# Linear attention with a two-part number format: the low half of v times the high half of A as 64-row matmuls

## The chip, the cores and the metric

The kernel runs on one core of a Trainium2 chip. The metric is the device time in microseconds (us). Lower is better. The engines are TensorE (PE, with its weight loads shown apart as PEld), VectorE (DVE), ScalarE (ACT), GpSimd (POOL) and SyncE (SP), which issues all the DMAs of this kernel.

## The reference

One transformer block on x of 4096 tokens x 512 numbers, in fp32:

```python
q = x @ Wq.T   # 16 heads of 128
k = x @ Wk.T   # 4 heads of 128, each shared by 4 heads of q
v = x @ Wv.T
q, k = rope(q), rope(k)
qf, kf = elu(q) + 1, elu(k) + 1
# causal linear attention, token by token:
state += kf[:, None] * v[None, :]
z += kf
out = (qf @ state) / (qf @ z + 1e-6)
x = layernorm(x + out @ Wo.T)
# feed-forward: Hadamard transform, up and gate projections, silu, Hadamard transform, down projection
x = layernorm(x + ffn(x))
```

## The kernel before

**Numbers in two parts.** Nearly every matmul is made of a high and a low part: `hi` is the value rounded to fp32r, the matmul format (an ACT copy, which rounds on writing), `lo` is the rest (a DVE subtraction). A product is then hi x hi + hi x lo + lo x hi, three matmuls that add up in one PSUM bank. The helper `hilo` (lines 89 to 91) does this for inputs and weights.

**Attention** (lines 134 to 488) runs over blocks of 256 tokens, 16 of them, twice: `s` is 0 or 1 and takes two of the four kv heads each time. So there are 32 blocks `n`; a block has two heads `g` and for each two slots `p` of 128 tokens, hence 128 slots `(n, g, p)`. A slot consists of two chunks `c2` of 64 tokens; `c = 2p + c2` is the chunk within its block. A chunk's 256 matmul columns are 4 heads of q times 64 tokens.

- `proj_v` (L192) projects v for a block, takes it out of PSUM as `vhl` (high part by ACT, L198; low part by DVE, L200), and copies it by DMA into `vd`: chunk by chunk, high and low part, once on partitions 0 to 63 and again on 64 to 127 (four DMAs, L202 to L205).
- `proj_k` projects k (L239), rotates it, applies elu + 1, and makes `khl`, the high and low part of each chunk next to each other: 64 columns of high, 64 of low. Column 0 of a chunk is replaced by z, the running sum (L267, L268).
- `proj_q` does the same for q, two heads of q at a time (`qh`, `ql`).
- `nat_k` and `state` transpose k (L277) and make the state before each of the four chunks. `state` (L289) has four matmuls in plain fp32, which the chip runs as two passes each. They take 64, 128, 64 and 128 partitions: the sum inside a pair of chunks starts at its first or second half.
- `scores` makes A, the products of k and q inside a chunk. One matmul has [high | low] of k as its 128 output partitions (L332), so that rows 0 to 63 of the bank get kh x qh and rows 64 to 127 kl x qh; a second one (L333) adds kh x ql to rows 0 to 63. ACT rounds rows 0 to 63 into A (L339), DVE computes what the rounding lost (`am`, L342) and adds it to rows 64 to 127 (L343). So A holds its high half on partitions 0 to 63 and its low half on 64 to 127. POOL then zeroes what lies above the diagonal, half by half (L346).
- `av` adds up the numerator of a slot in a PSUM bank `ps_num` (two banks): for each chunk three matmuls with the state (high x high, high x low, low x high), and two with `vd`. As A holds both halves on 128 partitions and `vd` holds the same v on both, one matmul gives vh x (Ah + Al), and a second vl x (Ah + Al) (L364). A further matmul with a selecting matrix adds up the denominator (`ps_den`, L367). ACT takes the numerator out (L370) and a DMA stores it.

The loop over slots (lines 420 to 486) starts `proj_q` five slots ahead and `scores` one slot ahead. That order is only a first one: the program is built with `tile.TileContext(nc, schedule_with_timeline_sim=True)`, and this scheduler reorders the instructions of every engine by what it reckons to be ready. Matmuls that stand next to each other in the source needn't do so in the program. Pools give the number of buffers: `A` has four, `vd` and `khl` two, `ps_num` two banks.

**After attention** come the output projection with the first layernorm (L622), and the feed-forward (L682 gate and up, L707 down) with the second.

Of the kernel before, what the change touches and what calls it, by code (L numbers as in the profile page):

```python
# [9 lines left out]
F32 = mybir.dt.float32  # L10
F32R = mybir.dt.float32r
# [36 lines left out]
def kernel(  # L48
# [8 lines left out]
    def dma(dst, src, pin=False):  # L57
        if dst.dtype == F32R:
            dst = dst.bitcast(F32)
        if src.dtype == F32R:  # L60
            src = src.bitcast(F32)
        i = nc.sync.dma_start(dst, src)
        if pin:
            tc.keep_in_program_order(i)
# [66 lines left out]
        dma(xn, x_n[t * 128:(t + 1) * 128])  # L131
        cur[t] = dict(nt=nt, rb=rb, xn=xn)

# [1 line left out]
    with ExitStack() as es:  # L135
        early = ExitStack()
        pe = early.enter_context(tc.tile_pool(name="ae", bufs=2, side="right"))
# [45 lines left out]
        def proj_v(n):  # L183
            s, b = divmod(n, NB)
            B = blk[n]
            ps = pmm.tile([128, 2, 256], F32, tag="mm", name="ps_v")
            for t in range(2):
                i = 0
                for k in range(4):
                    for xa, wa in (("xh", 0), ("xh", 1), ("xl", 0)):  # L190
                        w = W["v", s, k // 2][wa].rearrange("p (k d) -> p k d", k=2)
                        T.matmul(ps[:, t], B[xa][:, k, t * 128:(t + 1) * 128], w[:, k % 2],  # L192
                                 start=i == 0, stop=i == 11)
                        i += 1
            v32 = pe.tile([128, 2, 256], F32, tag="v32", name="v32")
            S.activation(v32, ps, AF.Copy)
            vhl = p1.tile([128, 2, 2, 256], F32R, tag="vhl", name="vhl")
            S.activation(vhl[:, 0], ps, AF.Copy, scale=rowm_s)  # L198
            yield
            V.scalar_tensor_tensor(vhl[:, 1], ps, rowm_s, vhl[:, 0].bitcast(F32), ALU.mult, ALU.subtract)  # L200
            vd = p2.tile([128, 2, 4, 256], F32R, tag="vd", name="vd")
            for half in range(2):  # L202
                for par in range(2):
                    dst = vd[half * 64:half * 64 + 64].rearrange("p l (t r) d -> p l t r d", r=2)[:, :, :, par]
                    dma(dst, vhl[par * 64:par * 64 + 64])  # L205
            vs = p1.tile([128, 2, 256], F32, tag="vs", name="vs")
            dma(vs[63:128], v32[0:65])
            dma(vs[0:63, 1], v32[65:128, 0])
            if b:
                dma(vs[0:63, 0], blk[n - 1]["v32"][65:128, 1])  # L210
            else:
                G.memset(vs[0:63, 0], 0.0)
            B.update(v32=v32, vd=vd, vs=vs)
# [30 lines left out]
        def proj_k(n):  # L244
            s, b = divmod(n, NB)
            B = blk[n]
            ps = proj(n, [("k", s, 0), ("k", s, 1)])
            kft = pe.tile([128, 2, 320], F32, tag="kft", name="kft")
            yield from rope(ps, B["csb"], kft[:, :, 64:320])
            if b:  # L250
                S.activation(kft[:, :, 0:64], blk[n - 1]["kft"][:, :, 256:320], AF.Copy)
            else:
                G.memset(kft[:, :, 0:64], 0.0)
            khl = p2.tile([128, 2, 4, 2, 64], F32R, tag="khl", name="khl")
            kh, kl = khl[:, :, :, 0], khl[:, :, :, 1]
            kc = kft[:, :, 64:320].rearrange("p g (c j) -> p g c j", c=4)
            S.activation(kh, kc, AF.Copy)
            yield
            V.tensor_tensor(kl, kc, kh.bitcast(F32), ALU.subtract)
            z = p2.tile([128, 2, 4], F32, tag="z", name="z")  # L260
            dz = p2.tile([128, 2, 4], F32, tag="dz", name="dz")
            for g in range(2):
                V.tensor_reduce(dz[:, g], kft[:, g, 1:257].rearrange("p (c j) -> p c j", c=4),
                                AX.X, ALU.add)
                V.tensor_tensor_scan(z[:, g], ones4, dz[:, g], blk[n - 1]["z"][:, g, 3:4] if b else 0.0,
                                     ALU.mult, ALU.add)
            V.tensor_copy(kh[:, :, :, 0], z)  # L267
            V.tensor_tensor(kl[:, :, :, 0], z, kh[:, :, :, 0].bitcast(F32), ALU.subtract)  # L268
            B.update(kft=kft, z=z, khl=khl)

        def nat_k(n):
# [50 lines left out]
        def scores(j):  # L322
# [5 lines left out]
            for c2 in range(2):  # L328
                c = 2 * p + c2
                t = slice(64 * c, 64 * c + 64)  # L330
                khl = B["khl"][:, g, c]
                T.matmul(ps[:, c2], khl.rearrange("p l j -> p (l j)"), qh[:, :, t], start=True, stop=True)  # L332
                T.matmul(ps[0:64, c2], khl[:, 0], ql[:, :, t], start=False, stop=True,  # L333
                         skip_group_check=True)
            am = p2.tile([64, 512], F32, tag="am", name="am")
            A = p3.tile([128, 2, 256], F32R, tag="A", name="A", bufs=4)
            Af = A.rearrange("p a b -> p (a b)")
            psf = ps.rearrange("p a b -> p (a b)")
            S.activation(Af[0:64], psf[0:64], AF.Copy)  # L339
            B["A", g, p] = A  # L340
            yield
            V.tensor_tensor(am, psf[0:64], Af[0:64].bitcast(F32), ALU.subtract)  # L342
            V.tensor_tensor(Af[64:128], psf[64:128], am, ALU.add)  # L343
            for h in range(2):
                ah = Af[64 * h:64 * h + 64].rearrange("p (a q) -> p a q", q=64)
                G.affine_select(ah, ah.bitcast(F32), pattern=[[0, 8], [1, 64]], compare_op=ALU.is_ge,  # L346
# [2 lines left out]
        def av(n, g, p):  # L349
            s, b = divmod(n, NB)  # L350
            B = blk[n]
            A = B.pop(("A", g, p))
            qh, ql = B["q", g]
            sh, sl, _ = B["S"][g]
            gs = slice(g * 128, (g + 1) * 128)
# [1 line left out]
                B["den", g] = pden.tile([4, 256], F32, tag="den", name="ps_den")  # L357
            den = B["den", g]
            ps = pnum.tile([128, 2, 256], F32, tag="num", name="ps_num")
            for c2 in range(2):  # L360
                c = 2 * p + c2
                t = slice(64 * c, 64 * c + 64)
                ops = [(sh[:, c], qh[:, :, t]), (sh[:, c], ql[:, :, t]), (sl[:, c], qh[:, :, t]),
                       (B["vd"][:, 0, c, gs], A[:, c2]), (B["vd"][:, 1, c, gs], A[:, c2])]  # L364
                for i, (l, r) in enumerate(ops):
                    T.matmul(ps[:, c2], l, r, start=i == 0, stop=i == len(ops) - 1)  # L366
                T.matmul(den, selr[:, c], A[:, c2], start=c == 0, stop=c == 3)  # L367
            gg = 2 * s + g
            num = p3.tile([128, 4, 2, 64], F32, tag="num", name="num")
            S.activation(num.rearrange("p h c q -> p c h q"),  # L370
                         ps.rearrange("p c (h q) -> p c h q", h=4), AF.Copy)
            dma(num_d[2 * b + p][:, gg], num.rearrange("p h c q -> p (h c q)"))
            if p == 1:
                ds = pout.tile([4, 256], F32, tag="ds", name="ds", bufs=2)
                S.activation(ds, den, AF.Copy, bias=EPS_DEN)
# [161 lines left out]
        rs = rsqrt_small(nc, pool, vv, tag)  # L537
        V.tensor_scalar(o, x, mv[:, 0:1], rs, ALU.subtract, ALU.mult)

# [1 line left out]
    with ExitStack() as es:  # L541
        p2 = es.enter_context(tc.tile_pool(name="c2", bufs=2, reuse_waits="tile"))
        p1 = es.enter_context(tc.tile_pool(name="c1", bufs=1, reuse_waits="tile"))
# [101 lines left out]
        late["s"].close()  # L645
    Y.clear()

# [1 line left out]
    with ExitStack() as es:  # L649
        p2 = es.enter_context(tc.tile_pool(name="f2", bufs=2, reuse_waits="tile"))  # L650
        p6 = es.enter_context(tc.tile_pool(name="f6", bufs=8, reuse_waits="tile"))
# [121 lines left out]
```

## Time and profile before

| | |
|---|---|
| median of 3 runs | 2405.66 us (2404.91 to 2408.99) |
| span of the profiled execution | 2408.2 us |
| mean granted TensorE clock | 0.990 |
| PE busy | 2356.0 us (98%), 13600 matmul records |
| DVE, ACT, POOL busy | 1825.2, 1106.5, 848.6 us |
| attention stage | 0 to about 940 us |
| output projection, feed-forward | from 941 us, from about 1317 us |

The profile shows one execution. For its time there is the span, from the first to the last instruction; a device time of that execution by itself isn't listed. The span lies within the times of the runs. Busy is the share of time in which an engine has an instruction under way. For TensorE it is no measure of pace, because matmuls overlap: one 256-column matmul has a record of 0.28 us, but the next one starts 0.113 to 0.118 us after it. Names are read as out<-in; `L366` is line 366 of the kernel.

### The profile page before, as it was taken

To read this page: it belongs to the slowest core of one execution; us is meant where nothing else is said; L and a number is where in the kernel's file an instruction comes from. 1 tells how busy PE (TensorE), PEld (TensorE's weight loads), DVE (VectorE), ACT (ScalarE), POOL (GpSimd) and SP (SyncE) were. 2 spreads that over 40 slices of the span, in tenths; PEclk is the share of its full clock that TensorE was granted. 3 is DMA by queue.
4 is the path that set the end of the run, shared out by engine and by line. 5 is a ranking of instruction groups with operands and counts; after the bars stand their busy time and mean duration, and the time that the engine had idled before them with its cause. 6 is when DMAs were issued, how large, how long until landed. Compare 5 with 4: busy or idle time off the path is not lost.

```text
span 2408.2 us, 38221 instructions
## 1 busy us (share of the span) xinstructions
PE 2356.0 (98%) x13600; PEld 2040.2 (85%) x13600; DVE 1825.2 (76%) x3408; ACT 1106.5 (46%) x1928; POOL 848.6 (35%) x839
## 2 busy tenths in 40 slices
PE   7999999999999998999999899999999999999998
PEld 6999999999999996777888688888888888888887
DVE  6999999998888897999998847475655757475443
ACT  5777777777777774222222332314141323324140
POOL 2455454454444452684242504022220405031000
PEclk9999999999999998999999899999999999999999
DMA  6555555644554447878885532213131222223120
GB/s 181 144 157 147 176 145 151 170 132 133 140 146 137 125 135 244 285 235 274 272 275 176 177 131 76 92 60 98 44 114 59 91 70 88 83 70 95 42 92 18
DMA packets 223583, 329.97 MB, mean 137 GB/s; under 512 B 62398, under 2 KB 99328, under 8 KB 219424
## 3 DMA queue, kind: packets, MB, share of 16 engines
q1 hardware_dynamic: 223392, 327.53, 44.6%
q8 instruction: 107, 1.75, 0.3%
q14 instruction: 84, 0.69, 0.1%
HBM read 209.62 MB, written 76.02 MB: 119 GB/s over the span
## 4 chain that ended last, share of the span: by engine, by line
PE 89%; DVE 6%; DMA 2%; issue 2%; ACT 1%; POOL 0%; SPq 0%; DVEq 0%; ACTq 0%; POOLq 0%
PE ps_gu L682 28%; PE ps_qk L239 16%; PE ps_dn L707 15%; PE ps_wo L622 12%; PE ps_num L366 6%; PE ps_s L289 4%; PE ps_v L192 3%; PE ps_sc L332 1%; PE ps_den L367 1%; PE ps_sc L333 1%; DMA rb<-rec_d 1%; DVE ps_on L552 1%; PE ps_tr L518 1%; DVE fw L510 1%; PE pt L277 0%
## 5 line engine op out<-in xcount | busy, mean ns | idle before, releaser
L682 PE MATMUL ps_gu<-yTh,wug_s 128*128 128x512 f32 x2048 | 646.4, 392 | 9.8 <-DVE wug_s L91 4.1
L682 PEld LDWEIGHTS ps_gu<-yTh,wug_s 128*128 128x128 f32 x2048 | 385.8, 189 | 95.3 <-DVE wug_s L91 8.6
L682 PE MATMUL ps_gu<-yTl,wug_s 128*128 128x512 f32 x1024 | 400.6, 391 | 0.0
L239 PE MATMUL ps_qk<-xh,wh 128*128 128x256 f32 x1280 | 358.7, 280 | 5.7 <-ACT wh L90 3.9
L239 PE MATMUL ps_qk<-xl,wh 128*128 128x256 f32 x1280 | 357.0, 279 | 0.6 <-DVE xl L91 0.6
L239 PE MATMUL ps_qk<-xh,wl 128*128 128x256 f32 x1280 | 357.2, 279 | 0.0
L346 POOL TENSOR_SCALAR_AFFINE_SELECT A<-A 64x512 fp32r<-64x512 f32 x256 | 219.9, 859 | 315.5 <-DVE am L342 208.8
L707 PE MATMUL ps_dn<-wdn,hh_h 128*128 128x512 f32 x1024 | 327.9, 396 | 0.0
L688 DVE SCALAR_TENSOR_TENSOR hh<-ps_gu,wsc,sg 128x512 f32<-128x512 f32 x128 | 95.9, 749 | 269.1 <-PE ps_gu L682 267.9
L221 POOL TENSOR_TENSOR sw<-sw,csb 128x512 f32<-128x512 f32 x160 | 217.2, 1358 | 166.8 <-ACT sw L220 158.5
L90 ACT ACTIVATE wug_s<-raw 128x512 fp32r<-128x512 f32 x256 | 150.5, 626 | 230.2 <-PE ps_gu L682 192.9
L239 PEld LDWEIGHTS ps_qk<-xh,wh 128*128 128x128 f32 x1280 | 242.4, 189 | 6.9 <-ACT wh L90 4.1
L504 POOL TENSOR_TENSOR fw<-y,suug 128x512 f32<-128x512 f32 x18 | 25.1, 1393 | 633.2 <-DMA y<-y_d 603.1
L239 PEld LDWEIGHTS ps_qk<-xl,wh 128*128 128x128 f32 x1280 | 241.9, 189 | 1.8 <-DVE xl L91 0.8
L239 PEld LDWEIGHTS ps_qk<-xh,wl 128*128 128x128 f32 x1280 | 241.7, 189 | 1.1
L707 PEld LDWEIGHTS ps_dn<-wdn,hh_h 128*128 128x128 f32 x1024 | 191.6, 188 | 43.7
L682 PEld LDWEIGHTS ps_gu<-yTl,wug_s 128*128 128x128 f32 x1024 | 193.5, 189 | 40.4
L687 ACT ACTIVATE sg<-ps_gu,wsc 128x512 f32<-128x512 f32 x128 | 87.7, 686 | 264.5 <-PE ps_gu L682 264.0
L622 PE MATMUL ps_wo<-wh,ol 128*128 128x512 f32 x512 | 203.9, 398 | 1.7 <-DVE ol L91 1.7
L622 PE MATMUL ps_wo<-wh,oh 128*128 128x512 f32 x512 | 203.3, 397 | 2.2 <-ACT oh L90 2.2
L622 PE MATMUL ps_wo<-wl,oh 128*128 128x512 f32 x512 | 202.8, 396 | 0.0
L707 PE MATMUL ps_dn<-wdn,hh_l 128*128 128x512 f32 x512 | 202.1, 395 | 0.0
(122 smaller groups left out, 5116.3 us busy)
## 6 DMA issues: line engine op xcount, KB each, us to landing
raw<-in_wug_dram SPq DMA_DIRECT2D x256, 256.0 KB
vd<-vhl SPq DMA_DIRECT2D x128, 256.0 KB
num_d<-num SPq DMA_DIRECT2D x128, 256.0 KB
rb<-rec_d SPq DMA_DIRECT2D x128, 256.0 KB
nt<-num_d SPq DMA_DIRECT2D x31, 1024.0 KB
y<-y_d SPq DMA_DIRECT2D x36, 256.0 KB
raw<-in_x_t_dram SPq DMA_DIRECT2D x32, 256.0 KB
csb<-in_cs_dram SPq DMA_DIRECT2D x32, 256.0 KB
```

What stands on the lines that cost most here:

```text
L90: S.activation(hi, src, AF.Copy)
L192: T.matmul(ps[:, t], B[xa][:, k, t * 128:(t + 1) * 128], w[:, k % 2], start=i == 0, stop=i == 11)
L221: G.tensor_tensor(sw, sw, sinb, ALU.mult)
L239: T.matmul(ps[:, j], W[key][wa][:, k * 128:(k + 1) * 128], B[xa][:, k], start=i == 0, stop=i == 11)
L289: T.matmul(ps[:, i], B["kfn"][r, g, i // 2], B["vs"][r, i // 2, g * 128:(g + 1) * 128], start=True, stop=True)
L346: G.affine_select(ah, ah.bitcast(F32), pattern=[[0, 8], [1, 64]], compare_op=ALU.is_ge, fill=0.0, base=0, channel_multiplier=-1)
L366: T.matmul(ps[:, c2], l, r, start=i == 0, stop=i == len(ops) - 1)
L622: T.matmul(ps, l[:, h], r, start=i == 0, stop=i == 47)
L682: T.matmul(ps, w[:, wa, u, k], ya[:, k], start=i == 0, stop=i == 11)
L687: S.activation(sg, pu[0], AF.Silu, scale=wsc[:, 1, it:it + 1])
L688: V.scalar_tensor_tensor(hh, pu[1], wsc[:, 0, it:it + 1], sg, ALU.mult, ALU.mult)
L707: T.matmul(ps, l[:, ts], r, start=i == 0, stop=i == 47)
```

## The change

The low part of v is multiplied with the high half of A only, and so by a matmul of 64 rows of the array. To let two of these stand side by side in the array, in rows 0 to 63 and 64 to 127, the second slot of each pair (p = 1) stores A with its halves swapped: low half on partitions 0 to 63, high half on 64 to 127. For that, `khl` of chunks 2 and 3 holds [low | high]: it is a list of twelve places of 64 columns, of which `kh` takes 0, 3, 6, 9 and `kl` 1, 4, 5, 8, so that a chunk's two places are neighbours either way. In the second slot kh x ql is added to what are now the rows of the low half.

In `av` the first call (p = 0) leaves its bank open; the second call ends with four 64-row matmuls, chunk by chunk and bank by bank: bank 0 with rows 0 to 63, bank 1 with rows 64 to 127, and the same for the second chunk. Then both banks are taken out and stored. `vd` keeps the high part of v on both halves of the partitions and only two places per half for the low part, filled by eight smaller DMAs. The copies and subtractions that make `khl` are split by head. A bank's first matmul alone has the start flag.

```diff
@@ -198,11 +198,12 @@
             S.activation(vhl[:, 0], ps, AF.Copy, scale=rowm_s)
             yield
             V.scalar_tensor_tensor(vhl[:, 1], ps, rowm_s, vhl[:, 0].bitcast(F32), ALU.mult, ALU.subtract)
-            vd = p2.tile([128, 2, 4, 256], F32R, tag="vd", name="vd")
+            vd = p2.tile([128, 6, 256], F32R, tag="vd", name="vd")
             for half in range(2):
                 for par in range(2):
-                    dst = vd[half * 64:half * 64 + 64].rearrange("p l (t r) d -> p l t r d", r=2)[:, :, :, par]
-                    dma(dst, vhl[par * 64:par * 64 + 64])
+                    dst = vd[half * 64:half * 64 + 64, 0:4].rearrange("p (t r) d -> p t r d", r=2)[:, :, par]
+                    dma(dst, vhl[par * 64:par * 64 + 64, 0])
+                    dma(vd[half * 64:half * 64 + 64, 4 + par], vhl[par * 64:par * 64 + 64, 1, half])
             vs = p1.tile([128, 2, 256], F32, tag="vs", name="vs")
             dma(vs[63:128], v32[0:65])
             dma(vs[0:63, 1], v32[65:128, 0])
@@ -251,12 +252,15 @@
                 S.activation(kft[:, :, 0:64], blk[n - 1]["kft"][:, :, 256:320], AF.Copy)
             else:
                 G.memset(kft[:, :, 0:64], 0.0)
-            khl = p2.tile([128, 2, 4, 2, 64], F32R, tag="khl", name="khl")
-            kh, kl = khl[:, :, :, 0], khl[:, :, :, 1]
-            kc = kft[:, :, 64:320].rearrange("p g (c j) -> p g c j", c=4)
-            S.activation(kh, kc, AF.Copy)
-            yield
-            V.tensor_tensor(kl, kc, kh.bitcast(F32), ALU.subtract)
+            khl = p2.tile([128, 2, 12, 64], F32R, tag="khl", name="khl")
+            kh = khl.rearrange("p g (o i) j -> p g o i j", o=2)[:, :, :, 0:6:3]
+            kl = khl[:, :, 1:9].rearrange("p g (o i) j -> p g o i j", o=2)[:, :, :, 0:4:3]
+            kc = kft[:, :, 64:320].rearrange("p g (o i j) -> p g o i j", o=2, i=2)
+            for g in range(2):
+                S.activation(kh[:, g], kc[:, g], AF.Copy)
+            yield
+            for g in range(2):
+                V.tensor_tensor(kl[:, g], kc[:, g], kh[:, g].bitcast(F32), ALU.subtract)
             z = p2.tile([128, 2, 4], F32, tag="z", name="z")
             dz = p2.tile([128, 2, 4], F32, tag="dz", name="dz")
             for g in range(2):
@@ -264,8 +268,9 @@
                                 AX.X, ALU.add)
                 V.tensor_tensor_scan(z[:, g], ones4, dz[:, g], blk[n - 1]["z"][:, g, 3:4] if b else 0.0,
                                      ALU.mult, ALU.add)
-            V.tensor_copy(kh[:, :, :, 0], z)
-            V.tensor_tensor(kl[:, :, :, 0], z, kh[:, :, :, 0].bitcast(F32), ALU.subtract)
+            zc = z.rearrange("p g (o i) -> p g o i", o=2)
+            V.tensor_copy(kh[:, :, :, :, 0], zc)
+            V.tensor_tensor(kl[:, :, :, :, 0], zc, kh[:, :, :, :, 0].bitcast(F32), ALU.subtract)
             B.update(kft=kft, z=z, khl=khl)
 
         def nat_k(n):
@@ -328,19 +333,22 @@
             for c2 in range(2):
                 c = 2 * p + c2
                 t = slice(64 * c, 64 * c + 64)
-                khl = B["khl"][:, g, c]
-                T.matmul(ps[:, c2], khl.rearrange("p l j -> p (l j)"), qh[:, :, t], start=True, stop=True)
-                T.matmul(ps[0:64, c2], khl[:, 0], ql[:, :, t], start=False, stop=True,
+                khl = B["khl"][:, g]
+                first = (0, 3, 5, 8)[c]
+                T.matmul(ps[:, c2], khl[:, first:first + 2].rearrange("p l j -> p (l j)"), qh[:, :, t],
+                         start=True, stop=True)
+                T.matmul(ps[0:64, c2], khl[:, 3 * c], ql[:, :, t], start=False, stop=True,
                          skip_group_check=True)
-            am = p2.tile([64, 512], F32, tag="am", name="am")
+            am = p2.tile([128, 512], F32, tag="am", name="am")
             A = p3.tile([128, 2, 256], F32R, tag="A", name="A", bufs=4)
             Af = A.rearrange("p a b -> p (a b)")
             psf = ps.rearrange("p a b -> p (a b)")
-            S.activation(Af[0:64], psf[0:64], AF.Copy)
+            rh, rl = slice(64 * p, 64 * p + 64), slice(64 - 64 * p, 128 - 64 * p)
+            S.activation(Af[rh], psf[rh], AF.Copy)
             B["A", g, p] = A
             yield
-            V.tensor_tensor(am, psf[0:64], Af[0:64].bitcast(F32), ALU.subtract)
-            V.tensor_tensor(Af[64:128], psf[64:128], am, ALU.add)
+            V.tensor_tensor(am[rh], psf[rh], Af[rh].bitcast(F32), ALU.subtract)
+            V.tensor_tensor(Af[rl], psf[rl], am[rh], ALU.add)
             for h in range(2):
                 ah = Af[64 * h:64 * h + 64].rearrange("p (a q) -> p a q", q=64)
                 G.affine_select(ah, ah.bitcast(F32), pattern=[[0, 8], [1, 64]], compare_op=ALU.is_ge,
@@ -349,7 +357,7 @@
         def av(n, g, p):
             s, b = divmod(n, NB)
             B = blk[n]
-            A = B.pop(("A", g, p))
+            A = B["A", g, p]
             qh, ql = B["q", g]
             sh, sl, _ = B["S"][g]
             gs = slice(g * 128, (g + 1) * 128)
@@ -357,19 +365,29 @@
                 B["den", g] = pden.tile([4, 256], F32, tag="den", name="ps_den")
             den = B["den", g]
             ps = pnum.tile([128, 2, 256], F32, tag="num", name="ps_num")
+            B["num", g, p] = ps
             for c2 in range(2):
                 c = 2 * p + c2
                 t = slice(64 * c, 64 * c + 64)
                 ops = [(sh[:, c], qh[:, :, t]), (sh[:, c], ql[:, :, t]), (sl[:, c], qh[:, :, t]),
-                       (B["vd"][:, 0, c, gs], A[:, c2]), (B["vd"][:, 1, c, gs], A[:, c2])]
+                       (B["vd"][:, c, gs], A[:, c2])]
                 for i, (l, r) in enumerate(ops):
-                    T.matmul(ps[:, c2], l, r, start=i == 0, stop=i == len(ops) - 1)
+                    T.matmul(ps[:, c2], l, r, start=i + c2 == 0, stop=False, skip_group_check=c2 > 0)
                 T.matmul(den, selr[:, c], A[:, c2], start=c == 0, stop=c == 3)
+            if p == 0:
+                return
+            for c2 in range(2):
+                for h in range(2):
+                    r = slice(64 * h, 64 * h + 64)
+                    T.matmul(B["num", g, h][:, c2], B["vd"][r, 4 + c2, gs], B["A", g, h][r, c2], start=False, stop=True,
+                             skip_group_check=c2 > 0)
             gg = 2 * s + g
-            num = p3.tile([128, 4, 2, 64], F32, tag="num", name="num")
-            S.activation(num.rearrange("p h c q -> p c h q"),
-                         ps.rearrange("p c (h q) -> p c h q", h=4), AF.Copy)
-            dma(num_d[2 * b + p][:, gg], num.rearrange("p h c q -> p (h c q)"))
+            for h in range(2):
+                num = p3.tile([128, 4, 2, 64], F32, tag="num", name="num")
+                S.activation(num.rearrange("p h c q -> p c h q"),
+                             B.pop(("num", g, h)).rearrange("p c (h q) -> p c h q", h=4), AF.Copy)
+                dma(num_d[2 * b + h][:, gg], num.rearrange("p h c q -> p (h c q)"))
+                B.pop(("A", g, h))
             if p == 1:
                 ds = pout.tile([4, 256], F32, tag="ds", name="ds", bufs=2)
                 S.activation(ds, den, AF.Copy, bias=EPS_DEN)
```

In the rest of the diff only three comment lines are blanked. From L198 on the line numbers move: the 64-row matmul is L382 of the changed kernel, the other matmuls of `av` are L375 and L376, those of `state` L294, of `scores` L338 and L340, of the projections of q and k L240.

## The prediction

> **What bounds the kernel now.** I read the page's head and engine sums first, then the busy share by slice, then the chain that ended last, and then windows over the attention stage, where the change lies (0 to 940 us; 75 us of it are fill and tail).
>
> ```profile
> span 2408.2 us, 38221 instructions
> PE 2356.0 (98%) x13600; PEld 2040.2 (85%) x13600; DVE 1825.2 (76%) x3408; ACT 1106.5 (46%) x1928; POOL 848.6 (35%) x839
> ...
> PE 7999999999999998999999899999999999999998
> PEld 6999999999999996777888688888888888888887
> DVE  6999999998888897999998847475655757475443
> ...
> PE 89%; DVE 6%; DMA 2%; issue 2%; ACT 1%; POOL 0%; SPq 0%; DVEq 0%; ACTq 0%; POOLq 0%
> ```
>
> TensorE is the chain (89%). In the attention stage (slices 1 to 15) PE and its weight loads are both at 9 tenths or more. The windows say the same more sharply (columns: stretch, length, then PE, PEld, DVE, ACT, POOL busy, granted clock, DMA share, GB/s):
>
> ```profile
> 62.00:900.00 838.00, 834.62 (x6801) 795.00 (x6800) 760.48 (x1279) 628.85 (x1121) 412.35 (x393) 1.00 0.52 146
> 900.00:940.00 40.00, 31.15 (x195) 26.92 (x194) 30.93 (x50) 22.51 (x43) 19.50 (x21) 0.83 0.66 196
> ```
>
> From 62 to 900 us PE lacks 3.4 us of the whole stretch. So there every ns that PE gains or loses goes into the time, and the other engines have room (DVE 78 us). Only the tail, 900 to 940, has waits.
>
> Busy is not rate, so I went to the order of matmuls in time. A 256-column matmul starts 0.113 to 0.118 us after the one before. A short stretch shows what rows of the array cost (start, length of the record, line, out<-in, rows*columns of the array in use):
>
> ```profile
> 698.40 0.28 PE L239 MATMUL ps_qk<-xl,wh 128*128 128x256 f32 x1
> 698.52 0.28 PE L239 MATMUL ps_qk<-xh,wl 128*128 128x256 f32 x1
> 698.72 0.48 PE L289 MATMUL ps_s<-vs,kfn 64*128 64x128 f32 x2
> 699.14 0.39 PE L332 MATMUL ps_sc<-qh,khl 128*128 128x256 f32 x1
> 699.36 0.28 PE L333 MATMUL ps_sc<-ql,khl 128*64 128x256 f32 x1
> ```
>
> ```profile
> 701.49 0.28 PE L367 MATMUL ps_den<-A,selr 128*4 128x256 f32 x1
> 701.61 0.38 PE L289 MATMUL ps_s<-vs,kfn 128*128 128x128 f32 x2
> 701.74 0.36 PE L366 MATMUL ps_num<-qh,sh 128*128 128x256 f32 x1
> 701.95 0.28 PE L366 MATMUL ps_num<-ql,sh 128*128 128x256 f32 x1
> ```
>
> The same line, L289, is two records of 128 columns both times. With 128 rows it takes 701.95 - 701.49 = 0.46 us from the matmul before it to the second after it, which is four ordinary steps (0.118 + 0.107 + 0.107 + 0.118 = 0.45). With 64 rows the same distance is 699.36 - 698.52 = 0.84 us. **A stretch of 64-row matmuls between 128-row ones costs 0.40 us beyond its work**: 0.09 of waiting before the new weights may load, 0.11 for that load lying bare, and the same on the way back. It is not the type (the 128-row case is the same fp32) and not the columns (L333 has 64 columns and goes at full pace). The trace has 128 such stretches: two for each of the 64 calls of `state`.
>
> **What the Trainium skill says.** TensorEngine Tiling (Array Packing), section Key Properties: "Changing tiling mode (not just tile) drains the TensorE". The trace agrees; its price is the 0.40 us for in and out. TensorE: Matmul & The Clock Gate, section LDWEIGHTS: loading time follows the columns, not the rows. The trace agrees: the 64-row loads of L289 take 187 ns in the mean, the 128-row ones 189, so a 64-row matmul by itself is no cheaper. The same page, Part 3: matmuls in different row groups can run at once. No run here shows it, since all 64-row matmuls of before sit in rows 0 to 63.
>
> **The change, part by part.**
>
> (a) Matmuls. Removed: the second `vd` matmul, 256 of 128 rows. Added: 256 of 64 rows, two per slot. The count is equal, so without overlap within pairs the work is equal: 0.
>
> (b) Pairs. They save at most two steps of four for each of 64 (block, group) pairs, 64 x 2 x 0.115 = 14.7 us, if the four stand as written: bank 0, bank 1, bank 0, bank 1. But the scheduler orders PE by what is ready. In the order that it gives the changed program, they stand so in 10 of the 64 only. In the other 54 the two matmuls of one bank come together, mostly right after that bank's own `den` matmul, and the other two follow 8 to 69 matmuls later: 108 twos in one row group, which can't overlap. (The same reading of the order for the kernel before gives the trace's order at all 13344 matmuls, so I trust it.) Gain: 10 x 2 x 0.115 = 2.3 us at most, 0 at least; weight loads at one per 0.107 us speak for little. I take 1.1.
>
> (c) Changes of rows. In that order I count where 64 follows 128. With 118 groups of new matmuls there would be 118 more stretches, but in 28 places the group runs straight into a 64-row L289 and shares its stretch. So 128 becomes 218: **90 more stretches x 0.40 = 36.0 us**, on PE, in a stage where PE has no slack. By block: 6 stretches in most early blocks and 7 from the twelfth on, for 4 now.
>
> (d) `khl` is made in two halves: 32 more on ACT and on DVE. DVE: two of 128x256 (L300, 0.42) for one of 128x512 (L259, 0.70), +0.14 x 32 = 4.6 us; ACT by the same reasoning about 5. Both lie beside PE, with 78 and 209 us of room; uncovered they would cost these sums, less what PE's own growth gives back. 0.
>
> (e) `vd` is filled by 8 transfers for 4, and a quarter less data. SP's issue is 0.82 us each; at most 4 x 0.82 = 3.3 us more per block, if the smaller ones are no cheaper. SP issues for 13.7 us of a 27.9 us block, and `vd` is used in the next block: hidden. What queues behind them on SP are `x` loads with a block to spare and `num` stores: 0. **At the start** it is not hidden: in SP's new order all eight and a `vs` stand ahead of the fifth `Wq` tile, which was issued ahead of them at 19.06 us. It should leave near 25.5. PE now stands 3.92 us at 25.9 for the sixth tile; it will stand for the fifth instead, with about 12 matmuls (1.4 us) fewer done. Cost 0 to 5 us, I take 2.
>
> (f) `num` of both slots is stored in the second call, and A lives longer. In the new order a bank is reused 25 or more matmuls (2.8 us) after its last one, except in the last blocks, while the ACT copy takes 0.59: 0. A has four buffers and never needs a fifth: 0. `vl` times the low half of A is dropped: it is in (a).
>
> (g) The tail, 900 to 940, loses some 14 us to waits and to a halved clock:
>
> ```profile
> 914.80:925.00 10.20, 8.18 (x30) 6.47 (x30) 8.51 (x15) 4.61 (x9) 4.20 (x4) 0.50 0.92 243
> ```
>
> The order changes there, and whether the clock drops again depends on where PE pauses; a few of the 90 stretches may hide in waits. I bound it by -6 and +8 and take 0. The later stages keep nearly the same order: 0.
>
> Sum: 36.0 - 1.1 + 2 = +36.9 us. The profiled span is 2408.2 us, 2.5 above the median of the runs and within their 2404.91 to 2408.99; taken to the median, 2405.66 + 36.9 = **2442.5 us**.
>
> **Rivals.** 0.2% (4.8 us) is about what a measurement of this kernel can tell from no change.
>
> 1. Slower by the changes of rows: above. Chance 0.92, with a range of its own near the one below.
>
> 2. Faster: 64-row matmuls of the rounded type (fp32r) go in and out without the wait. All stretches of before are plain fp32, so this isn't excluded. Then the 36 us vanish, the ten foursomes give 2.3, and a tail without the halved clock up to 6: 2397 us. For it: packing is what the layout is made for. Against: the wait stands where the neighbours are fp32r, in both directions, and a 128-row fp32 matmul has none. It decides if a stretch costs under 0.04 us. Chance 0.05.
>
> 3. No change: the same, but with the start (+2) eating the foursomes' gain: 2405. Chance 0.03.
>
> 4. Much slower: each change of row group inside a foursome drains too, 10 x 3 x 0.2 = 6 us, and the start and tail go badly, +5 and +8: 2461. Part of case 1's upper end.
>
> That the pairs are not pairs is not a rival but what I forecast.
>
> **How the numbers follow.** Low end: 36.0 - 2.3 - 6 = +28, less 2 for stretches hidden in waits: 2431. High end: 36 + 5 + 8, and some of case 4: 2456. Cases 2 and 3 (0.08) and part of the far ends are left outside. Chances: faster 0.05, same 0.03, slower 0.92.
>
> **What would show it.** PE's busy sum grows by about the time lost, and the windows still show PE full. In the late blocks a period of 27.94 us becomes 27.94 + 3 x 0.40 = 29.15. The two new matmuls show 0.84 us from the matmul before to the second after. Stages from 1000 us on only shift. Wrong if: the new matmuls start within 0.12 us of their neighbours; or the foursomes' starts lie a few ns apart and the block time falls; or the added time stands in waits of PE on ACT, POOL or DMA.

## The result, and the profile after

The changed kernel takes 2431.76 us (median of 4 runs, 2430.67 to 2433.71); the kernel before, on the same chip, 2405.28 (2404.31 to 2408.99). The ratio is 1.0109, 95% interval 1.0095 to 1.0123: **slower by 26.5 us**. The forecast was slower by 36.9.

First the head of the page of the changed kernel, its engine sums, the slices of the three busiest engines and the chain that ended last:

```profile
span 2430.0 us, 38502 instructions
...
PE 2385.0 (98%) x13600; PEld 2037.1 (84%) x13600; DVE 1864.1 (77%) x3440; ACT 1113.8 (46%) x1960; POOL 852.1 (35%) x839
...
PE   7999999999999998999999899999999999999998
PEld 7999999999999996877888688888888888888887
DVE  7999999998888888999999847565565647475443
...
PE 77%; DVE 11%; DMA 3%; issue 3%; POOL 2%; ACT 2%; SPq 1%; DVEq 0%; ACTq 0%; POOLq 0%
```

PE has 29.0 us more busy time (2385.0 - 2356.0) for the same 13600 matmuls, DVE 38.9 us more. The chain's share of PE has fallen from 89 to 77%, DVE's has risen from 6 to 11: more of the steps that set the end lie on DVE. The windows over the attention stage (PE, PEld, DVE, ACT, POOL busy, clock, DMA share, GB/s):

```profile
62.00:900.00 838.00, 836.49 (x6608) 770.17 (x6608) 776.42 (x1278) 615.83 (x1116) 403.12 (x380) 1.00 0.45 132
900.00:940.00 40.00, 36.16 (x260) 31.14 (x258) 37.23 (x49) 30.55 (x54) 23.28 (x20) 0.96 0.47 131
```

In the same 838 us PE starts 193 matmuls fewer than before (6608 for 6801) while it looks busier (836.49 for 834.62 us). That is what bare drains look like: the next matmul starts some 0.22 us later instead of 0.115, and a record of 0.28 us or more covers that wait. Here is a pair of the new matmuls, L382, in the changed kernel's timeline (start, length, line, out<-in, rows*columns):

```profile
701.53 0.28 PE L376 MATMUL ps_den<-A,selr 128*4 128x256 f32 x1
701.75 0.50 PE L382 MATMUL ps_num<-A,vd 64*128 64x256 f32 x2
702.17 0.38 PE L240 MATMUL ps_qk<-xh,wh 128*128 128x256 f32 x1
702.39 0.28 PE L240 MATMUL ps_qk<-xl,wh 128*128 128x256 f32 x1
```

702.39 - 701.53 = 0.86 us from the matmul before to the second after, for four steps of 0.115: 0.40 us of drain, with the rounded type as with plain fp32. The two share one row group and follow one another.

**PE's ledger.** To say where time went I took all of PE's matmul records up to the first output projection (`ps_wo`), and from each distance between two starts took off the ordinary step (0.1155 us, 0.107 after a 128-column record). What is left over is a stretch's if a 64-row record is the one started or one of the two before it (with no idle time of 0.4 us or more there, and at the full clock), else a wait. "Counted" is all stretches x 0.40, less 0.23 (two steps) for each group of four in which matmuls of different row groups ran at once, two by two. The columns "start", "middle" and "tail" are the waits of the first 60 us, of the last 45, and between them; the last column is when the output projection begins.

| kernel | stretches | counted | stretches in the trace | start | middle | tail | first `ps_wo` |
|---|---|---|---|---|---|---|---|
| before | 128 | 51.2 | 50.7 | 19.3 | 10.4 | 18.4 | 941.3 |
| after | 218 | 81.9 | 82.3 | 16.8 | 4.9 | 18.9 | 965.4 |
| difference | +90 | +30.7 | **+31.6** | -2.5 | **-5.5** | +0.5 | +24.1 |

Two things blur these columns. Stretches at a halved clock stand in start and tail: 2.2 us before, 3.9 after. And the middle takes in by how much the ordinary steps lie off 0.1155 us: 3.0 us before and 0.9 after, from -2.9 to +7.6 in the kernels below. Such steps come in two lengths, 113 to 114 ns and 117 to 119 ns (72% and 26% of those from one `ps_qk` matmul to the next before); what decides between them stays open. The delays proper of the middle, those of over 20 ns (around fp32 and transposing matmuls over 40 ns by group), are 5.3 us before, without 0.8 us at a halved clock at 60 to 61.5 us, and 3.3 after.

The rest of the kernel, from the first `ps_wo` on, is 2.2 us shorter in this execution; 24.1 - 2.2 is, rounded, the difference of the spans, 21.8. The medians differ by 26.5. A span isn't the time of its run: the profiled execution of after has a span of 2430.0 us and took 2431.76, which is the median. With the same 1.8 us on top, the profiled execution of before (span 2408.2) took about 2410, an estimate. So it is no typical run, as the comparison of its span with the times of the runs made it look, but some 4.7 us above the median: 21.8 + 4.7 = 26.5. About 3 us of that seem to lie behind attention: from the first `ps_wo` on the profiled execution of before takes 1466.8 us, and that of a kernel with the same code there (the one with `khl` in halves, below, a run of 2405.50 us) 1463.8.

So stretches cost all that is lost and more, and the middle gives 5 us of it back. The theory to test: **a stretch costs 0.40 us wherever it stands, but PE isn't alone at the bound; a second chain, from scores through ACT, DVE and POOL to A and back to PE, stands a few us behind it.** Rivals: the loss is due to the pairs that the scheduler broke up; or to other parts of the change (`khl` in halves, banks held longer).

### The profile page after: what moved, and what is told of

The parts are those of the page before. It is cut to its first block, busy times and chain, and to the rows that moved or that the text cites. A ratio compares the mean times of both kernels' runs of the same rounds, so it can differ in the third digit from the quotient of the medians.

```text
span 2430.0 us, 38502 instructions
## 1 busy us (share of the span) xinstructions
PE 2385.0 (98%) x13600; PEld 2037.1 (84%) x13600; DVE 1864.1 (77%) x3440; ACT 1113.8 (46%) x1960; POOL 852.1 (35%) x839
## 4 chain that ended last, share of the span: by engine, by line
PE 77%; DVE 11%; DMA 3%; issue 3%; POOL 2%; ACT 2%; SPq 1%; DVEq 0%; ACTq 0%; POOLq 0%
PE ps_gu L700 28%; PE ps_dn L725 15%; PE ps_qk L240 12%; PE ps_wo L640 10%; PE ps_num L375 3%; PE ps_s L294 3%; PE ps_v L192 2%; PE ps_num L382 1%; DVE ps_qk L223 1%; DVE x L226 1%; DVE kft L230 1%; DMA rb<-rec_d 1%; PE ps_sc L338 1%; SPq L62 1%; PE ps_sc L340 1%
## 5 line engine op out<-in xcount | busy, mean ns | idle before, releaser
L700 PE MATMUL ps_gu<-yTh,wug_s 128*128 128x512 f32 x2048 | 646.2, 392 | 10.3 <-DVE wug_s L91 4.7
L240 PE MATMUL ps_qk<-xh,wh 128*128 128x256 f32 x1280 | 366.6, 286 | 4.1 <-ACT wh L90 3.7
L240 PE MATMUL ps_qk<-xh,wl 128*128 128x256 f32 x1280 | 359.7, 281 | 0.0
L354 POOL TENSOR_SCALAR_AFFINE_SELECT A<-A 64x512 fp32r<-64x512 f32 x256 | 229.1, 895 | 368.6 <-DVE am L350 250.3
L240 PE MATMUL ps_qk<-xl,wh 128*128 128x256 f32 x1280 | 357.3, 279 | 0.0
L240 PEld LDWEIGHTS ps_qk<-xh,wh 128*128 128x128 f32 x1280 | 242.1, 189 | 11.5 <-ACT wh L90 3.9
L240 PEld LDWEIGHTS ps_qk<-xh,wl 128*128 128x128 f32 x1280 | 241.7, 189 | 3.5
L240 PEld LDWEIGHTS ps_qk<-xl,wh 128*128 128x128 f32 x1280 | 242.2, 189 | 1.2
```

Source lines behind the costliest of these rows:

```text
L240: T.matmul(ps[:, j], W[key][wa][:, k * 128:(k + 1) * 128], B[xa][:, k], start=i == 0, stop=i == 11)
L700: T.matmul(ps, w[:, wa, u, k], ya[:, k], start=i == 0, stop=i == 11)
```

## Experiments

Ratios are to the kernel before, measured anew beside each group of experiments; its median was between 2406.1 and 2407.1 us.

### The changed layout without 64-row matmuls

```diff
-T.matmul(B["num", g, h][:, c2], B["vd"][r, 4 + c2, gs], B["A", g, h][r, c2], start=False, stop=True,
+T.matmul(B["num", g, h][:, c2], B["vd"][:, 4 + c2, gs], B["A", g, h][:, c2], start=False, stop=True,
```

> The changed kernel with its layout, transfers, order in the source and late store of the numerators kept, but the low product as 128-row matmuls: it takes in, besides low v times high A, the other slot's low v times the low half of A. In the scheduler's order 64 rows follow 128 in 128 places, as in the kernel before (218 in the changed one). Theory (changes of the number of rows cost 0.40 us per stretch of 64 rows): the whole loss goes, 2431.8 - 90 x 0.35 to 0.40 = 2396 to 2400 us, a little under the kernel before, since start and waits were better in the changed one. Rival (transfers, halved khl and banks held open cost the time): it stays at 2427 to 2432.

Measured: 2415.85 us (2412.54 to 2417.78), ratio 1.0037 [1.0024, 1.0049], between the two ranges. The ledger has 50.3 us of stretches, as before the change, so 32 us of them are gone; but the middle has 20.6 us for 4.9 (delays of over 20 ns alone: 14.0 for 3.3), and the end moves by 16. The changed layout costs some 9.6 us against the kernel before with no stretch more.

### The four matmuls as one block

The same kernel as changed, with the four 64-row matmuls of a pair of slots (a foursome) in a critical section of the scheduler (`with tc.tile_critical():`), so that nothing comes between them.

> The changed kernel with the four 64-row matmuls of a group held together by a critical section, so that all 64 groups stand as bank 0, bank 1, bank 0, bank 1. 178 stretches. Theory: +50 x 0.40 = +20 us of stretches against the kernel before, less two steps of 0.115 us in each of the 64 foursomes = -14.7, less some 5 of better start and waits as in the changed kernel: 2401 to 2412 us. Each foursome's second and fourth matmul starts within 10 ns of the one before. Rival (foursomes don't overlap in general): 2421 to 2430. Rival (with pairs intact the change is the gain it looks like): under 2400.

Measured: 2525.09 us, ratio 1.0495 [1.0481, 1.0509]: a miss by far. The waits of PE's weight loads show why (line waited for: us, times, longest):

```profile
PEld ps_num L383 <- issue: 85.9, 64, 7.1
```

64 times, once per foursome, PE stands until the section may begin, up to 7.1 us each, and the granted clock is halved 18 times in the execution, for 9 in the kernel before. The section acted as a barrier. The kernel's time tells nothing on the foursomes, but the ledger still does: 178 stretches with 64 foursomes are 178 x 0.40 - 64 x 0.23 = 56.5 us by count, and 56.7 in the trace.

### The four matmuls pinned

```diff
-T.matmul(B["num", g, h][:, c2], B["vd"][r, 4 + c2, gs], B["A", g, h][r, c2], start=False, stop=True,
-         skip_group_check=c2 > 0)
+tc.keep_in_program_order(
+    T.matmul(B["num", g, h][:, c2], B["vd"][r, 4 + c2, gs], B["A", g, h][r, c2], start=False,
+             stop=True, skip_group_check=c2 > 0))
```

> The changed kernel with each of the four 64-row matmuls pinned to its place in the program order, so that they stand as a foursome in all 64 (block, group) pairs instead of in 10. In the built order 64 follows 128 in 189 places (128 before the change, 218 after). By the price of a stretch: against the 128-row version of the changed layout (2415.8 us) 61 more stretches x 0.40 = +24.4 us and 64 foursomes x 0.23 = -14.7 us, so +10 on PE, of which some lies in waits that are there anyway: 2416 to 2428, still slower than before. The rival, that the loss comes from the pairs being broken up and that unbroken pairs pay: 2400 us or less.

Measured: 2435.76 us (2434.20 to 2436.81), ratio 1.0118 [1.0102, 1.0135]. The rival falls: with all 64 foursomes whole the kernel is no faster. A foursome in this kernel's timeline:

```profile
516.68 0.28 PE L376 MATMUL ps_den<-A,selr 128*4 128x256 f32 x1
516.89 0.50 PE L383 MATMUL ps_num<-A,vd 64*128 64x256 f32 x4
517.33 0.39 PE L240 MATMUL ps_qk<-xh,wl 128*128 128x256 f32 x1
517.55 0.28 PE L240 MATMUL ps_qk<-xh,wh 128*128 128x256 f32 x1
```

517.55 - 516.68 = 0.87 us: four matmuls in the time of the two above. In the median of 61 foursomes the second starts 3 ns after the first, the third at 225, the fourth at 227. So matmuls of different row groups do run side by side, as TensorE: Matmul & The Clock Gate of the Trainium skill has it in Part 3 and no run had shown before, and a foursome saves 0.23 us; but the way in and out costs 0.40. **Whole foursomes lose too.**

The time came out 8 us above the range. Up to the first `ps_wo` the sum is as reckoned: 963.0 us against 952.7 of the 128-row version, +10.3 for +10. The rest is in the join to the next stage, which takes 1471.2 us from there for 1463.4. PE's waits from 920 to 1012 us:

```profile
PE ps_wo L641 <- DVE ol L91: 8.4, 1, 8.4
PE ps_wo L641 <- ACT oh L90: 6.3, 1, 6.3
```

14.7 us for the first operands of the output projection; the 128-row version has 4.4 there. The expectation had left that stage out.

### Fewer stretches in the kernel before

```diff
-            for i in range(4):
+            for i in (0, 2, 1, 3):
```

in `state`: 64, 64, 128, 128 rows for 64, 128, 64, 128.

> The kernel before with one edit: the four state matmuls of a block and head in the order 0, 2, 1, 3, so that the two of 64 rows stand next to each other. The scheduler keeps 47 of 64 such pairs together: 81 stretches of 64 rows for 128. Theory: -47 x 0.40 = -18.8 us: 2384 to 2389 us. Rival (the wait at a stretch lies in a time in which PE would have waited for something else anyway): 2402 to 2407.

Measured: 2395.89 us (2395.36 to 2396.39), ratio 0.9956 [0.9941, 0.9972]. The stretches fall from 128 to 81 and their ledger by 18.1 us (50.7 to 32.6), as expected; but the middle grows from 10.4 to 19.1, and the kernel gains 10 us, between the two ranges.

### No stretches in the kernel before

```diff
+        vz = p1.tile([128, 2, 256], F32, name="vz")
+        G.memset(vz, 0.0)
...
+            G.tensor_copy(vz[0:64], vs[0:64])
...
-                r = slice(0, 64 * (i % 2) + 64)
-                T.matmul(ps[:, i], B["kfn"][r, g, i // 2], B["vs"][r, i // 2, g * 128:(g + 1) * 128],
+                T.matmul(ps[:, i], B["kfn"][:, g, i // 2], (B["vs"] if i % 2 else vz)[:, i // 2, g * 128:(g + 1) * 128],
```

The 64-row matmuls of `state` become 128-row ones whose lower half meets zeros (`num` gets two buffers, to make room).

> The kernel before without any 64-row matmul: the two state matmuls of 64 rows read 128 rows, with a copy of the shifted v whose rows 64 to 127 are zero (a POOL copy of 64x512 per block), and the numerator's SBUF tiles are two for three to make room. 0 stretches for 128. Theory: -128 x 0.40 = -51 us: 2352 to 2358 us if nothing else becomes the bound; DVE had 78 us of room in the attention stage, so 27 are left, and up to 15 us may be lost to new waits: 2352 to 2370. Rival (drain hides other waits): over 2385.

Measured: 2398.99 us (2396.70 to 2400.06), ratio 0.9967 [0.9955, 0.9979]. All 50.7 us of stretches are gone and only 7 us of time: the theory's range is missed by 29 us, and the rival's holds. The middle is 46.1 us now, about 3 of them at a halved clock (403.9 to 407.3 and 468.8 to 472.2 us). The top of PE's waits over the whole span, and the next of its weight loads':

```profile
PE ps_sc L334 <- DVE A L345: 13.4, 21, 1.5
PEld ps_num L368 <- POOL A L348: 12.7, 31, 1.9
```

A score matmul waits for the DVE addition that reads the score bank for the last time: the pool has one such bank, and the next slot's scores need it. The second line is the wait of `av` for the A that POOL has masked. In the kernel before they are 2.4 and 1.7 us. **This is the second bound**: both waits lie on the chain from scores to A and back.

### The same four with DVE relieved

Here `am` is left out: the two DVE passes that make the low half of A become one copy, for example `V.tensor_copy(Af[64:128], psf[64:128])`, and A lacks what the rounding of its high half lost. The four kernels are the one before, the changed one, its 128-row version, and the one without stretches.

> The kernel before without am, the rest that the rounding of A lost: the low half of A is copied from PSUM as it is, 128 subtractions less on VectorE (86 us of records). This leaves out a part of the low half of A. Theory (VectorE is the second bound of the attention stage, but not before PE): the waits of PE there, some 10 us, go in part: 2394 to 2404 us. Rival (VectorE has room): 2403 to 2409.

> The changed kernel without am, as above. 197 stretches in the scheduler's order, 46 foursomes and 36 twos. With VectorE relieved, stretches count in full: against the 128-row form without am +69 x 0.40 - 46 x 0.23 = +17 us: 2411 to 2422. Rival (stretches hide): within 8 us of the 128-row form without am.

> The changed layout with 128-row low matmuls, without am. 128 stretches, as in the kernel before without am. Theory (the 10 us that the layout lost against the kernel before are VectorE's: two halved khl subtractions and longer records): with VectorE relieved they go: within 4 us of the kernel before without am. Rival (they come of the transfers or of banks held open): 7 to 12 us above it.

> The kernel before without 64-row matmuls and without am. Theory (the stretches' 51 us came back as only 7 since PE then waits for VectorE): with VectorE relieved the gain comes: 45 to 52 us under the kernel before without am, 2345 to 2358. Rival (the gain is lost to something else, POOL or the chain from scores to A): 2380 to 2398.

| without `am` | us | ratio to before | stretches | counted | in the trace | middle |
|---|---|---|---|---|---|---|
| before | 2392.01 | 0.9938 [0.9923, 0.9953] | 128 | 51.2 | 51.3 | 3.2 |
| changed | 2413.16 | 1.0026 [1.0015, 1.0037] | 197 | 68.2 | 66.6 | 1.1 |
| changed, 128 rows | 2400.49 | 0.9973 [0.9961, 0.9985] | 128 | 51.2 | 49.0 | 6.0 |
| before, no stretches | 2374.64 | 0.9866 [0.9849, 0.9882] | 0 | 0 | 0 | 21.7 |

The first shows that the work on DVE does set time: 14 us gained with no stretch removed. How isn't parted: `am` is a link of the chain from scores to A as well as load, and of the 18.4 us by which the first `ps_wo` comes earlier, 9.0 lie in the tail and 5.6 in ordinary steps, which got 0.9 ns shorter. Between the second and third, 17.6 us of stretches are worth 12.7 us of time, where with `am` 32 were worth 16: with DVE lighter, a larger part of what PE saves arrives. The third is 8.5 us above the first, in the rival's range: the layout's cost isn't DVE's load alone. The last misses its range by 17 us. Its stretches are all gone and 17.4 us of that show; PE waits 10.0 us for the score bank again, which the smaller load left in place, and the first output projection 16 us for its operands.

### Which part of the layout costs 9.6 us

Two parts of the change, each put into the kernel before.

```diff
-            S.activation(kh, kc, AF.Copy)
+            for g in range(2):
+                S.activation(kh[:, g], kc[:, g], AF.Copy)
...
-            V.tensor_tensor(kl, kc, kh.bitcast(F32), ALU.subtract)
+            for g in range(2):
+                V.tensor_tensor(kl[:, g], kc[:, g], kh[:, g].bitcast(F32), ALU.subtract)
```

> The kernel before with one part of the change: the copies and subtractions that make khl are split by head, 32 more on ACT and on DVE; the layout of khl, A and the matmuls stay. The 128-row version of the changed layout is 9.6 us above the kernel before, with nothing in its stretches to account for it. If the cause is DVE's and ACT's extra work (priced at 0 in the prediction, 4.6 us of DVE if uncovered): 2410 to 2416. If it is the later end of the numerator banks and of A: 2404 to 2408. If it is neither (swapped layout, vd transfers): also 2404 to 2408, with the late version near before as well.

Measured: 2405.50 us (2402.88 to 2408.47, 13 runs), ratio 0.9993 [0.9984, 1.0001]. The halves cost nothing that can be measured, as the prediction's step (d) had it.

```diff
-                       (B["vd"][:, 0, c, gs], A[:, c2]), (B["vd"][:, 1, c, gs], A[:, c2])]
+                       (B["vd"][:, 0, c, gs], A[:, c2])]
...
+            if p == 0:
+                return
+            for c2 in range(2):
+                for h in range(2):
+                    T.matmul(B["num", g, h][:, c2], B["vd"][:, 1, 2 * h + c2, gs], B["A", g, h][:, c2], start=False,
+                             stop=True, skip_group_check=c2 > 0)
...
+            for h in range(2):
```

> The kernel before with another part of the change: the products of low v with A (128 rows as before, no swapped halves) wait for the second slot of a pair, so that bank and A of the first slot are held longer and both are taken out together. If this is the 9.6 us of the 128-row version: 2411 to 2418, with PE waiting for a ps_num bank or for A. If it is the halves of khl: 2404 to 2408. If the two share it: 2408 to 2412 each.

Measured: 2410.23 us (2406.30 to 2414.90, 21 runs), ratio 1.0015 [1.0009, 1.0022]: about 3 us (2 to 5 by the interval), with 18.2 us in the middle for 10.4; of these 7.8 more, 4.6 are ordinary steps that got longer. Holding banks and A until the second slot is about a third of the 9.6. If the parts add up, the other two thirds lie in what neither kernel has, the swapped halves, the eight `vd` transfers and the order that the scheduler makes of them. These weren't parted further. The transfers are suspect: from 60 to 900 us the weight loads of `state` in the 128-row version wait six times, 3.3 us in all, for `vs`, which SP issues among the `vd` transfers. The kernel before has no such wait.

### A faster kernel

The order 64, 64, 128, 128 again, and the low half of the state on POOL: `V.tensor_tensor(sl, ...)` becomes `G.tensor_tensor(sl, ...)`.

> The kernel before with two edits: the four state matmuls ordered 64, 64, 128, 128 rows (stretches 128 to 65), and the subtraction that makes the low half of the state on POOL instead of DVE. With the first alone 2395.9 us were measured, 18 us of stretches gone and 9 us of waits for DVE come in their place. If those waits are DVE's load, relieving it gives back some of them: 2380 to 2392. If they are the single score bank's chain through ACT, DVE and POOL, or POOL becomes late: 2394 to 2400.

Measured: **2380.28 us** (2377.89 to 2387.37), ratio 0.9894 [0.9878, 0.9910], faster than both kernels. Of the stretches 65 are left, 26.0 us by count and 26.0 in the trace, and the middle is 11.1 us, about what the kernel before has and 8 less than with the order alone. Engine sums of its page:

```profile
PE 2322.0 (98%) x13600; PEld 2020.9 (85%) x13600; DVE 1787.8 (75%) x3344; ACT 1104.1 (46%) x1928; POOL 943.9 (40%) x903
```

DVE has 37 us less than before, POOL 95 more, on an engine at 40%. With DVE relieved, what PE saves arrives: 24.7 us fewer in stretches, 26.8 less in time. As this subtraction is no link of the chain from scores to A, it points to DVE's load as what held the order's gain back. Not all of the step from 10 to 27 us is due to that, though: the scheduler also kept 16 stretches fewer (6.6 us) than with the order alone. The subtraction on POOL without the new order wasn't run.

## Why the prediction was right, and where it was off

**The direction and the mechanism (c).** The count of 218 stretches, read from the built order, is the trace's. The price of 0.40 us holds in every kernel: counted stretches and those traced at the full clock agree within 2.2 us in all of them, from 0 to 218 stretches. Rival 2 (fp32r goes in and out free) falls with the 0.86 us shown above. TensorEngine Tiling (Array Packing) of the Trainium skill, section Key Properties, says that changing the mode drains TensorE; here the drain is 0.40 us for in and out, whatever the type.

**Stretches in the sum: 34.9 forecast, 31.6 measured.** Steps (b) and (c) took overlap only inside the ten foursomes, which gave it in full (2.3 us, where 1.1 was taken). The trace has another: in 13 places a new matmul on rows 64 to 127 stands next to a `state` matmul on rows 0 to 63, and they start 4 to 7 ns apart. Such a group of four goes from its predecessor to the second after in 0.852 us, where the step had 1.08: 13 x 0.23 = 3 us. There is one such group in each late block, and most of why such a block, forecast at 29.15 us, takes 28.82.

**"Every ns that PE gains or loses goes into the time."** This is the sentence that failed. The ledger's middle is 5.5 us shorter in the changed kernel, where the prediction took 0. Not all of this is cover. 2.1 us are ordinary steps that got 0.35 ns shorter in the mean (116.0 to 115.7), for an unknown reason, and 0.8 us is the end of a halved clock at 60 to 61.5 us in the kernel before. The delays proper fell from 5.3 us to 3.3: **only about 2 us of the new stretches can lie in waits that were there anyway.** The windows had shown 3.4 us of room for that, as a wait shorter than the record of the matmul ahead of it (0.28 us, with the next start due after 0.116) isn't idle time. More cover went, it seems, to waits that the new layout brings: 14.0 us of delays in its 128-row version, 3.3 with the new stretches. (The scheduler's order differs between the two as well, so this isn't shown for certain.) The prediction had allowed up to 2 us for stretches hidden in waits at its low end, and took 0.

The time from the start of one block's first v projection to the next one's tells where which bound holds:

| us per block | blocks 2 to 12 | blocks 20 to 29 |
|---|---|---|
| before | 27.9 | 27.94 |
| after | 28.7 | 28.82 |
| changed layout, 128 rows | 28.7 | 27.9 |
| before, no stretches | 28.6 | 26.4 |
| the faster kernel | 27.1 | 27.0 |

In the late blocks PE sets the pace: taking all four stretches from a block gives 1.55 us, for 4 x 0.40 = 1.6. In the early blocks the kernel without stretches is slower than the one before, and the 128-row layout stands at the period that the changed kernel has with 0.80 us of stretches on top. There the other chain sets it, by the waits shown above: 15 of the 21 for the score bank lie from 141 to 373 us. The changed kernel hides the layout's cost under its stretches there, as far as the scheduler's order isn't the cause; so undoing them alone brought back 16 us and not 26.

**DVE, "room of 78 us".** Step (d) priced DVE's growth at 4.6 us. DVE's records in attention grew by 35 (910.9 to 946.1 us). The halves of `khl` are 6 of these. Most of the others are the same instructions taking longer. From 62 to 900 us, before (busy, mean ns | idle):

```profile
L320 DVE TENSOR_TENSOR ql<-sw,qh 128x512 fp32r<-128x512 f32 x120 | 118.0, 983 | 7.4 <-ACT qh L318 6.3
L229 DVE SCALAR_TENSOR_TENSOR kft<-sw,x 128x512 f32<-128x512 f32 x30 | 26.5, 883 | 0.1
```

and after:

```profile
L325 DVE TENSOR_TENSOR ql<-sw,qh 128x512 fp32r<-128x512 f32 x116 | 130.3, 1123 | 1.0
L230 DVE SCALAR_TENSOR_TENSOR kft<-sw,x 128x512 f32<-128x512 f32 x29 | 37.9, 1307 | 0.1
```

Same shape, 140 and 424 ns more each. The traces show what goes with it: with nothing under way on POOL such a record takes 680 ns in either kernel (`kft` 679 and 679, `ql` 685 and 683), with POOL at work for over half of it `kft` takes 1115 and 1981 ns in the mean, `ql` 1135 and 1183. The records of `x<-ps_qk,sw`, which read one operand from PSUM, don't lengthen (677 and 687 ns beside POOL). So a sum of DVE times from one order isn't carried over to another. Their cost in time stayed hidden in the changed kernel, as step (d) said, but as an even race, not with 78 us to spare: an engine that is 91% busy in the stage (760.48 of 838 us) and sits in a loop with one score bank has no free 9%.

**The start (e).** The shift is as described: eight `vd` transfers take 6.1 us of SP's issue for 4.0, the `Wq` tiles leave from 24.57 us on, and PE stands for one after the matmul started at 24.4 instead of 25.6. But two waits of before, 1.1 us for DVE's A (`ps_sc`, at 53.7 us) and 2.6 for x (`ps_v`, at 56.8), are not there in the new order. The start gained 2.5 where +2 was taken.

**The tail (g)** was taken at 0 and came at +0.5. The later stages were taken at 0 and came at -2.2, which says more of the profiled execution of before (3 us long there, above) than of the change.

Added up, forecast to measured, on the profiled executions: +36.9 less 3.3 (stretches), 5.5 (middle), 4.5 (start) and 2.2 (later), plus 0.5 (tail) makes +21.9, for +21.8. Against the medians it is 26.5, since the profiled execution of before ran 4.7 us above its median and that of after is the median.

**How near it was.** The measured 2431.76 us lies 0.8 above the low end of the range, and that low end rested in the main on 6 us from the tail, which gave nothing; only its 2 us of hidden stretches came about. What brought the time down besides was the overlap with `state`, the ordinary steps and the start. That the range still held is in part luck; the direction and the price of a stretch aren't.

## What to carry to other kernels

Count mode changes in the built order, not in the source, and price a packed pair with its way in and out: here 0.40 us of drain buys 0.23 us of overlap, so by these numbers a stretch has to hold four overlapping pairs (4 x 0.115 = 0.46 us) before it pays, an estimate that no run here tries. A wait that is shorter than the record ahead of it is no idle time in a profile; reckon slack from the distances between starts, and treat an engine at 90% in a loop with a single buffer as a bound. When an edit shortens the bounding engine, relieve the one next to it in the same edit: the reordered state was worth 10 us alone and 27 with DVE lighter (and 16 stretches fewer). And compare a span with spans, not with the times of runs.

## What the runs showed of the hardware

- Four 64-row fp32r matmuls, two row groups by two banks, start at 0, 3, 225 and 227 ns: the time of two. Plain fp32 of one line on rows 0 to 63 and fp32r of another on rows 64 to 127 run side by side as well (0.852 us for the group).
- A change of rows costs the same 0.40 us for 64-row matmuls of both types, and doesn't grow if four stand in the stretch: 0.86 us for a two and for a foursome.
- DVE records of one shape took 883 ns in one order of the program and 1307 in another. With POOL idle beside them they took 679 ns in both.
